# A selective-scan and spectral-filter kernel: z by halves in the turns' PSUM bank, conv ahead of it, later state copies, an own buffer for single h tiles, the image loaded first

## The chip, the core and the metric

The kernel runs on one core of one Trainium2 chip. The metric is the device time of one execution in microseconds (us); smaller is better. Three executions of the kernel before took 7441.77, 7444.82 and 7446.32 us, so its median is 7444.82 us. One more execution was profiled.

## The reference, cut to what matters

Two layers follow each other on x of shape 4 x 128 x 128 x 128 (batch, channel, height, width), all in float32. The first layer is a selective scan over the 16,384 pixels of each image:

```python
h1 = relu(xf @ mlp_w1.T + mlp_b1);  xm = h1 @ mlp_w2.T + mlp_b2
x_in, z = split(xm @ in_proj_w.T)                 # 256 channels each
u = silu(causal_conv(x_in, conv_w) + conv_b)      # 4 taps, depthwise
dt, B, C = split(u @ x_proj_w.T)                  # 8, 16, 16
delta = softplus(dt @ dt_proj_w.T + dt_proj_b)
h = h * exp(delta * A) + delta * B * u            # 16 states for each channel, step by step
y = (sum over states of h * C) + u * D
out = (y * silu(z)) @ out_proj_w.T
x1 = silu(group_norm(out)) + x
```

The second layer computes four softmax weights for each image from a normalised 1x1 convolution of x1, and filters x1 with a weighted sum of four spectral filters in the Fourier domain. It is matrix products with DFT matrices here, and the change doesn't touch its loop.

## The kernel before, in words

**Stages.** `block0` does the first layer and, for images 0 to 2, the softmax weights; `block1` does the rest. By the trace the scans of `block0` run from 61.0 to 6614.4 us, so what follows is `block1` and takes some 830 us.

**Chunks, units, slots.** `block0` cuts the four images into 128 chunks of 512 pixels. The 256 channels x 16 states of a chunk are 32 scans of 128 rows x 512: 8 units (`u`, numbered 0 to 7 in a chunk; two halves j of the channels, four rotations r) of four scans p = 0 to 3. Two scans are a pair and take one slot; a chunk is 16 slots. A unit's even slot scans p = 0 and 1 and its odd slot p = 2 and 3.

**One unit.** GpSimd makes `hb` = delta u B for p = 1 to 3 (`dbu`, L358); TensorE turns p = 0 into PSUM bank `b0` (L378); ScalarE makes the decay tiles `da0` to `da3` by Exp (`exps`, L391; `da1` to `da3` have one PSUM bank each, `da0` two SBUF buffers); VectorE runs the four scans (L409). For p = 2 and 3 VectorE scans in place in `da` and multiplies by C itself (L411). For p = 0 and 1 it scans into an SBUF tile `h` of two rows, of which there are two buffers, and GpSimd multiplies by C (L416). In a few units the share differs by `by_vector`: in the chunks in which the last image is normalised (48 of 128, "norming" chunks), GpSimd also takes p = 2 of unit 6, which needs an `h` tile in which one row is used; in every other of the remaining chunks VectorE takes p = 1 of unit 6. ScalarE copies the last state of each scan for the next chunk (L412 out of `da`, L417 out of `h`). TensorE sums `hb` over the states into `y` (L430).

**The order.** Nothing is scheduled automatically: `todo[slot, phase]` lists functions, and the program is written slot by slot, phase by phase, so each engine's queue is that order. `pre(k)` gives the slots of the steps that prepare chunk k, relative to the start of the chunk before it. Those that matter here, with their slots in a chunk:

- 9: `h1_mm`, 10: `h1_act`, 11: `xm_mm`, 12: `xm_act` (of the chunk after the next)
- 13 (written -3): `z_mm`, two products (L220) into two banks of the PSUM pool `psp`, which has two banks; 15 (-1): `z_act`, two copies (L225)
- 0 and 1: `cv_mm(0)`, `cv_mm(1)`, the convolution as 4 products each (L231; 8 in the profile, since a float32 product shows as two), in `psp`
- 2: `silu_act`: Silu of the convolution to `u` (L236, two instructions) and of z (L237, one)
- 3: `xd_mm` (L242) into the bank `pt`; 4: `xd_act`; 5: `dt_mm`; 6: `dt_act`, Softplus (L270); 5 to 14: turns of `du` in `pt` and `bt_act` (L299)

`pt` is the "turns' bank", a pool of one bank, `turn_bank`. Exp, Silu and Softplus need different tables, so ScalarE loads a table ahead of `silu_act`, ahead of `dt_act`, and ahead of the exps after each. `exps(n)` stands in slot n - 1. `dt_act` and `silu_act` stand between the exps of one unit's p = 2, 3 and the exps of the next unit's p = 0, 1.

**Start.** Twenty-five constants are loaded by L75 alternately on SyncE's and ScalarE's queues, and the taps (L124), before anything else; the first image tile (L191) follows on SyncE's queue, in memory that the taps had held.

**Images done.** `finish` normalises image b and computes its weights while image b + 1 is scanned; the last agg tiles (i from 28 on) use the turns' bank in slot 15 (`agg_mm`, L597, and `agg_act`, L601).

Of the kernel before, what the change touches and what calls it, by code (L numbers as in the profile page):

```python
# [33 lines left out]
P = 128  # L34
# [10 lines left out]
@with_exitstack  # L45
def kernel(ctx: ExitStack, tc: tile.TileContext, a: dict, out: bass.AP):
    nc = tc.nc
    x = a["x"]
    B, C, H, W = x.shape
    L = H * W  # L50
    NCH = L // T
    DI = a["mlp_w1T"].shape[1]
    NH = DI // P
    NS = (a["x_wT"].shape[1] - a["dt_wT"].shape[0]) // 2
    NG = NS // SQ
    ND = P // DG
    R = a["dt_wT"].shape[0]
    NX = R + 2 * NS
    KC = a["conv_wT"].shape[0]
    HALO = KC - 1  # L60
    WF = W // 2 + 1
    NF = a["wg_wT"].shape[1]

    cpool = ctx.enter_context(tc.tile_pool(name="const", bufs=1))
    dpool = ctx.enter_context(tc.tile_pool(name="dram", bufs=1, space=DRAM))
    spool = ctx.enter_context(tc.tile_pool(name="stats", bufs=2))
    opool = ctx.enter_context(tc.tile_pool(name="outs", bufs=2, space=DRAM))

    loads = [0]

    def const(name, shape, src):
        t = cpool.tile(shape, F32, tag=name, name=name)
        eng = (nc.sync, nc.scalar)[loads[0] % 2]
        loads[0] += 1
        eng.dma_start(out=t, in_=src)  # L75
        return t

    def col(name):

        n = a[name].shape[0] // P  # L80
        return const(name, [P, n], a[name].rearrange("(j p) -> p j", p=P))

    w1 = const("w1", [P, DI], a["mlp_w1T"])
    b1 = col("mlp_b1")
    w2 = const("w2", [P, NH, C], a["mlp_w2T"].rearrange("(j p) c -> p j c", p=P))
    b2 = col("mlp_b2")
    win = const("win", [P, 2 * DI], a["in_wT"])
    cb = col("conv_b")
    wx = const("wx", [P, NH, NX], a["x_wT"].rearrange("(j p) r -> p j r", p=P))
    wdt = const("wdt", [R, DI], a["dt_wT"])  # L90
    bdt = col("dt_b")
    alog = const("alog", [P, NH * NG * ND], a["alog_q"])
    sel = const("sel", [P, DG], a["c_sel"])
    dvec = col("D")
    wo = const("wo", [P, NH, C], a["out_wT"].rearrange("(j p) c -> p j c", p=P))
    gnw = col("gn_w")
    gnb = col("gn_b")
    ident = const("ident", [P, P], a["c_ident"])
    g0 = const("g0", [P, P], a["c_g0"])
    g1 = const("g1", [P, P], a["c_g1"])  # L100
    gam = col("gn_gamma")
    bet = col("gn_beta")
    wagg = const("wagg", [P, 2, C], a["agg_wT"].rearrange("(j p) o -> p j o", p=P))
    bagg = col("agg_b")
    wwg = const("wwg", [P, NF], a["wg_wT"])
    bwg = const("bwg", [P, NF], a["wg_b"].partition_broadcast(P))
    resw = const("resw", [P, 1], a["residual_weight"].partition_broadcast(P))

    eps = cpool.tile([P, 1], F32, tag="eps", name="eps")
    nc.vector.memset(eps, EPS)  # L110
    ones = cpool.tile([P, P], F32, tag="ones", name="ones")
    nc.vector.memset(ones, 1.0)

    amat = cpool.tile([P, NH * NG * ND], F32, tag="amat", name="amat")
    nc.scalar.activation(amat, alog, AF.Exp)
    nc.vector.tensor_scalar_mul(amat, amat, -1.0)
    diag = cpool.tile([P, NH, P], F32, tag="diag", name="diag")
    for j in range(NH):
        nc.vector.tensor_scalar_mul(diag[:, j, :], ident, dvec[:, j : j + 1])

    wck = cpool.tile([P, KC, DI], F32, tag="wck", name="wck")
    with tc.tile_pool(name="taps", bufs=1) as taps:
        cwb = taps.tile([P, KC, DI], F32, tag="cwb", name="cwb")
        nc.sync.dma_start(out=cwb, in_=a["conv_wT"].partition_broadcast(P))  # L124
        for t in range(KC):
            nc.vector.tensor_mul(wck[:, t, :], win[:, 0:DI], cwb[:, t, :])

    weff0 = cpool.tile([P, C], F32, tag="weff0", name="weff0")
    nc.vector.tensor_scalar_mul(weff0, wagg[:, 0, :], gam[:, 0:1])
    nc.vector.scalar_tensor_tensor(weff0, wagg[:, 1, :], gam[:, 1:2], weff0, ALU.mult, ALU.add)  # L130
    bias0 = cpool.tile([P, 1], F32, tag="bias0", name="bias0")
    wts = [cpool.tile([P, NF], F32, tag=f"wts{b}", name=f"wts{b}") for b in range(B)]

    x1 = [dpool.tile([C, H, W], F32, tag=f"x1_{b}", name=f"x1_{b}") for b in range(B)]
    x1flat = [t.rearrange("c h w -> c (h w)") for t in x1]
    xflat = x.rearrange("b c h w -> b c (h w)")

    stats, outs = {}, {}
    shared = SimpleNamespace(**{k: v for k, v in locals().items() if k not in ("ctx", "tc")})
    block0(tc, shared)  # L140
    block1(tc, shared)


def block0(tc, s):
# [4 lines left out]
    with ExitStack() as ctx:  # L149
# [18 lines left out]

        pb0 = psum("bias0")
        for j in range(2):  # L170
            nc.tensor.matmul(pb0[:, 0:1], s.wagg[:, j, :], s.bet[:, j : j + 1], start=j == 0, stop=j == 1)
        nc.vector.tensor_add(s.bias0, pb0[:, 0:1], s.bagg)

        st = {}
# [6 lines left out]
        def pre(k):  # L181
# [7 lines left out]
            def load():  # L189
                xt = d["xt"] = p1.tile([P, T], F32, tag="xt", name=f"xt_{k}")  # L190
                nc.sync.dma_start(out=xt, in_=s.xflat[b, :, i * T : (i + 1) * T])  # L191

# [22 lines left out]

            def z_mm():
                for j in range(NH):
                    ps["z", j] = psum(f"z_{k}_{j}")
                    w = s.win[:, DI + j * P : DI + (j + 1) * P]
                    nc.tensor.matmul(ps["z", j], w, d["xm"][:, HALO:], start=True, stop=True)  # L220

            def z_act():
                d["zs"] = p2.tile([P, NH, T], F32, tag="zs", name=f"zs_{k}", bufs=3)
                for j in range(NH):
                    nc.scalar.copy(d["zs"][:, j, :], ps["z", j])  # L225

# [83 lines left out]
            def rep_load(j):  # L310
# [7 lines left out]
                (-9, "pe", load), (-7, "pe", h1_mm), (-6, "act", h1_act), (-5, "pe", xm_mm), (-4, "act", xm_act),  # L318
                (-3, "pe", z_mm), (-1, "act", z_act), (0, "pe", partial(cv_mm, 0)), (1, "pe", partial(cv_mm, 1)),
                (2, "act", silu_act), (3, "pe", xd_mm), (4, "act", xd_act), (5, "pe", dt_mm), (5, "pe", xd_turn),  # L320
# [72 lines left out]
        def scans(n):  # L393
# [8 lines left out]
            last = d["last", j, r, p] = tiny.tile([P, 2], F32, tag=f"st{j}_{r}_{p}", name=f"st_{k}_{j}_{r}_{p}")  # L402
            if pool:
                h = p2.tile([P, 2, T], F32, tag="h", name=f"h_{k}_{j}_{r}_{p}")
            for q in range(2):
                b = hb[:, p + q, :] if p + q else d.pop("b0")
                init = 0.0 if k % NCH == 0 else st[k - 1]["last", j, r, p][:, q : q + 1]
                o = das[q] if q in dve else h[:, q, :]
                nc.vector.tensor_tensor_scan(o, das[q], b, init, ALU.mult, ALU.add)  # L409
# [3 lines left out]
            if pool:  # L413
                q = slice(pool[0], pool[-1] + 1)
                ps = slice(p + pool[0], p + pool[-1] + 1)
                nc.gpsimd.tensor_tensor(hb[:, ps, :], h[:, q, :], d["C"][:, ps, :], ALU.mult)  # L416
                nc.scalar.copy(last[:, q], h[:, q, T - 1])  # L417

# [47 lines left out]
        for k in range(n_chunks):  # L466
            for at, phase, f in pre(k) + post(k):
                todo[at + (k - 1) * NP, phase].append(f)
        io = SimpleNamespace(big=p2, bufs=3, small=tiny, psum=psum)

# [4 lines left out]
        def agg(i):  # L475
# [3 lines left out]
            c = i * NP  # L479
            return c + 9, c + 15, c + 15, turn_bank  # L480

# [12 lines left out]
        with tc.manual_schedule():  # L494
            for n in range(min(slots), max(slots) + 1):
                for phase in ("turn", "sums", "pe", "exps", "act", "pool", "dbu", "gate", "scans", "dve", "end"):
                    for f in todo[n, phase]:
# [3 lines left out]
def group_norm(s, io, b, mat, which, stat, at, then):  # L501
# [12 lines left out]
    def mean_mm():  # L514
        ps = g["ps"] = io.psum(f"gm_{which}_{b}")
        nc.tensor.matmul(ps[:, 0:1], mat, g["mv"][:, 0:1], start=True, stop=True)

# [7 lines left out]
    def var_mm():  # L525
        ps = g["ps"] = io.psum(f"gv_{which}_{b}")
        nc.tensor.matmul(ps[:, 0:1], mat, g["q"], start=True, stop=True)

# [13 lines left out]
def finish(s, io, b, first, norm, agg):  # L542
# [89 lines left out]

    todo = group_norm(s, io, b, s.g0, 0, lambda: stats[b], first, start)
    for i in range(NCH):
# [5 lines left out]
    c = at[2] + 5  # L640
    todo += group_norm(s, io, b, s.g1, 1, lambda: g["stat"], c, middle)
    todo += [(c + 4, "pe", bias_mm), (c + 4, "act", bias_act)]
    for i in range(NCH):
        at = agg(i)
        todo += [
            (at[0], "dve", partial(agg_load, i)), (at[1], "pe", partial(agg_mm, i, at[3])),
            (at[2], "act", partial(agg_act, i)),
        ]
# [321 lines left out]
```

## Time and profile before

| what | value |
|---|---|
| median of 3 executions | 7444.82 us (7441.77 to 7446.32) |
| profiled execution, its own time | 7446.74 us |
| its span, first to last instruction | 7445.0 us |
| mean granted TensorE clock | 0.875 |
| first scan starts, last scan ends | 60.97, 6614.41 us |
| first h1 product starts (L196) | 17.08 us |
| chunks 12 to 15, first scan to first scan | 49.62, 51.15, 50.42, 50.20 us |
| a norming chunk (34 to 48), first scan to first scan | 52.0 us |

The profile's engines are PE (TensorE matmul), PEld (its weight loads), DVE (VectorE), ACT (ScalarE), POOL (GpSimd) and SP (SyncE). In a timeline row stand the start, the time it took, engine, line, operation, output <- inputs, shapes and count, and in brackets the idle time of the engine before it with the instruction that is taken to have released it. Where an instruction waits for several semaphores, the profile names the one that came last by its records, which may be another's. Vector instructions overlap a little: a scan is 1.26 us long, but the next starts 1.18 us after it; a product is 0.67 us long and the next starts 0.59 us after it.

### The profile page before, as it was taken

The numbers are of one execution on the slowest core, as the hardware profiler recorded it, in microseconds if no ns is written. First come the engines' busy times: TensorE is split into PE (matmuls) and PEld (weight loads), VectorE is DVE, ScalarE is ACT, GpSimd is POOL, SyncE is SP. The second block draws the span as 40 slices with busy tenths as digits, with TensorE's granted clock in tenths as the row PEclk, the third lists the DMA queues.
The fourth block names the chain that finished last, engine by engine and source line by source line (L and its number), as shares of the span: only waits on it lengthen the run. The fifth ranks groups of instructions, "written<-read, shape, count | busy, mean of one in ns | idle before, by whom it ended". The sixth has DMA issues, their size and how long they took to land.

```text
span 7445.0 us, 90541 instructions
## 1 busy us (share of the span) xinstructions
PE 6005.7 (81%) x25908; PEld 2664.1 (36%) x25908; DVE 7031.4 (94%) x8168; ACT 6328.6 (85%) x13181; POOL 6900.6 (93%) x3188
## 2 busy tenths in 40 slices
PE   7787878877778788887777788877777788867999
PEld 2223223322222233332222223232222233237999
DVE  6999999999999999999999999999999999977787
ACT  6888888888888888888888888888888888866887
POOL 6999999999999999999999999999999999976788
PEclk8888888888888888888888889988888889889999
DMA  4444444444554544544545454445554554547665
GB/s 138 159 154 150 151 156 156 143 161 168 174 188 164 179 165 156 169 166 169 184 168 185 161 171 166 159 165 175 171 188 166 173 169 151 173 149 216 177 185 155
DMA packets 853767, 1242.06 MB, mean 167 GB/s; under 512 B 76680, under 2 KB 308240, under 8 KB 853264
## 3 DMA queue, kind: packets, MB, share of 16 engines
q1 hardware_dynamic: 851152, 1236.11, 50.3%
q8 instruction: 204, 3.34, 0.2%
q14 instruction: 299, 2.45, 0.1%
q10 hardware_dynamic: 2112, 0.16, 0.0%
HBM read 992.71 MB, written 243.27 MB: 166 GB/s over the span
## 4 chain that ended last, share of the span: by engine, by line
ACT 20%; DVE 19%; PE 17%; POOL 9%; issue 8%; DMA 5%; SPq 1%; DVEq 0%; ACTq 0%; POOLq 0%
DVE da L409 8%; ACT da L391 8%; DVE h L409 6%; PE pp_cv L231 5%; ACT bt L299 4%; POOL hb L358 4%; POOL hb L416 4%; DVE hb L411 3%; DMA dd<-delta 2%; PE y L430 2%; PE pa L776 1%; ACT L391 1%; PE px L790 1%; PE px L791 1%; POOL du L307 1%
## 5 line engine op out<-in xcount | busy, mean ns | idle before, releaser
L358 POOL TENSOR_TENSOR hb<-rdu,rB 128x1536 f32<-128x1536 f32 (+2 forms) x1536 | 3607.6, 2365 | 16.2 <-DMA rdu<-dd 16.2
L416 POOL TENSOR_TENSOR hb<-h,rC 128x1024 f32<-128x1024 f32 (+1 forms) x1072 | 2438.7, 2277 | 279.8 <-DVE h L409 263.0
L391 ACT ACTIVATE da<-rdelta,amat 128x512 f32<-128x512 f32 x4096 | 2674.6, 696 | 9.2 <-ACT st L412 0.2
L409 DVE TENSOR_TENSOR_SCAN da<-da,st,hb 128x512 f32<-128x512 f32 x1976 | 2420.3, 1268 | 7.1 <-ACT da L391 7.0
L378 PE MATMUL b<-ident,bt 128*128 128x128 f32 x4096 | 768.9, 311 | 767.9 <-DVE h L409 633.0
L430 PE MATMUL y<-hb,sel 128*32 128x512 f32 x8192 | 1364.0, 743 | 4.8 <-POOL hb L416 2.9
L409 DVE TENSOR_TENSOR_SCAN h<-da,st,b 128x512 f32<-128x512 f32 x992 | 1261.3, 1271 | 111.4 <-POOL hb L358 37.5
L411 DVE TENSOR_TENSOR hb<-da,rC 128x512 f32<-128x512 f32 x2040 | 1296.7, 674 | 3.0
L409 DVE TENSOR_TENSOR_SCAN h<-da,st,hb 128x512 f32<-128x512 f32 x1000 | 1252.7, 1256 | 1.3 <-ACT da L391 1.3
L299 ACT ACTIVATE bt<-pt_dut,xdt 128x256 f32<-128x256 f32 x2048 | 1194.6, 708 | 46.8 <-PE pt_dut L288 46.5
L231 PE MATMUL pp_cv<-xm,wck 128*128 128x512 f32 x2048 | 1111.7, 692 | 9.8 <-ACT zs L225 9.7
L378 PEld LDWEIGHTS b<-ident,bt 128*128 128x128 f32 x4096 | 532.0, 156 | 1341.4 <-DVE h L409 997.1
L412 ACT COPY st<-da 128x1 f32<-128x1 f32 x2040 | 295.8, 173 | 567.9 <-DVE hb L411 562.6
L231 PEld LDWEIGHTS pp_cv<-xm,wck 128*128 128x128 f32 x2048 | 438.4, 226 | 771.1 <-issue 502.8
L755 POOL TENSOR_TENSOR wb<-wb,term 128x1040 f32<-128x1040 f32 x192 | 460.9, 2401 | 157.2 <-ACT term L749 147.2
L288 PE MATMUL pt_dut<-ident,du 128*128 128x128 f32 x1024 | 214.1, 337 | 280.5 <-ACT st L412 271.4
L426 PE MATMUL y<-u,diag 128*128 128x512 f32 x512 | 291.0, 651 | 156.8 <-DVE zs L440 155.6
L307 POOL TENSOR_TENSOR du<-delta,u 128x512 f32<-128x512 f32 x256 | 319.0, 1267 | 37.5 <-ACT delta L270 37.5
L417 ACT COPY st<-h 128x2 f32<-128x2 f32 (+1 forms) x1072 | 214.7, 200 | 162.8 <-DVE h L409 154.6
L288 PEld LDWEIGHTS pt_dut<-ident,du 128*128 128x128 f32 x1024 | 134.1, 164 | 578.6 <-POOL du L307 419.2
L196 PE MATMUL pp_h<-xt,w 128*128 128x512 f32 x512 | 296.6, 707 | 51.7 <-DMA xt<-in_x 46.6
L391 ACT ACT_TABLE_LOAD x261 | 334.9, 1283 | 2.9
(137 smaller groups left out, 8019.0 us busy)
## 6 DMA issues: line engine op xcount, KB each, us to landing
rdelta<-dd SPq DMA_DIRECT2D x1024, 256.0 KB, 3.6
rdu<-dd SPq DMA_DIRECT2D x1024, 256.0 KB, 4.6
rC<-bc SPq DMA_DIRECT2D x512, 256.0 KB, 5.1
rB<-bc SPq DMA_DIRECT2D x384, 256.0 KB, 3.5
dd<-delta SPq DMA_DIRECT2D x256, 256.0 KB, 5.3
dd<-du SPq DMA_DIRECT2D x256, 256.0 KB, 4.5
ft<-in_filt_w SPq DMA_DIRECT2D x96, 520.0 KB, 7.1
xt<-in_x SPq DMA_DIRECT2D x128, 256.0 KB, 5.5
```

The costliest lines, as they stand in the source:

```text
L231: nc.tensor.matmul(ps["cv", j], w, d["xm"][:, t : t + T], start=t == 0, stop=t == KC - 1)
L288: nc.tensor.transpose(ps["dut"][:, 2 * t + j, :], d["du"][:, j, at : at + P], s.ident)
L299: nc.scalar.activation(d["bt"][:, 2 * h + t, :, :, q], src, AF.Copy, scale=d["xdt"][:, 2 * h + t, R + q : R + q + 1])
L307: nc.gpsimd.tensor_tensor(du, d["delta"][:, j, :], d["u"][:, j, :], ALU.mult)
L358: nc.gpsimd.tensor_tensor(hb[:, p : p + n, :], d["du", j][:, m : m + n, :], d["B"][:, p - 1 : p - 1 + n, :], ALU.mult)
L378: nc.tensor.transpose(b[:, t * P : (t + 1) * P], src, s.ident)
L391: nc.scalar.activation(d["da", p][q], d["delta", j][:, m, :], AF.Exp, scale=s.amat[:, c : c + 1])
L409: nc.vector.tensor_tensor_scan(o, das[q], b, init, ALU.mult, ALU.add)
L411: nc.vector.tensor_tensor(hb[:, p + q, :], das[q], d["C"][:, p + q, :], ALU.mult)
L416: nc.gpsimd.tensor_tensor(hb[:, ps, :], h[:, q, :], d["C"][:, ps, :], ALU.mult)
L430: nc.tensor.matmul(y[m * DG : (m + 1) * DG, :], s.sel, d["hb", j, r][:, p, :], start=False, stop=r == NG - 1)
L755: nc.gpsimd.tensor_tensor(wb, wb, u[n].terms[f], ALU.add)
```

## The change

- `z_mm` and `z_act` are split into halves j. Both halves use the turns' bank, one after the other: `z_mm(0)` in slot 15, `z_act(0)` in slot 0, `z_mm(1)` in slot 1, `z_act(1)` in slot 2 ahead of `silu_act`. `cv_mm(0)` moves from slot 0 to 13, `cv_mm(1)` from 1 to 15, ahead of `z_mm(0)`.
- The copies of last states out of `h` (L417) go to a phase "late" of the next slot, behind that slot's exps. Those out of `da` (L412) stay.
- An `h` tile of one row gets a buffer `h1` of its own, and the ring of two keeps the tiles of two rows.
- All constants are loaded on SyncE's queue. The first image tile is loaded on ScalarE's, behind `w1` in the program; then come the constants and products that the scan needs (the first slot's end), in slot 4 those of the normalisation, in slot 8 the products made of these. The taps are loaded into `wck` and multiplied in place.
- The agg steps in the turns' bank move from slot 15 to the end of slot 0 of the next chunk.
- The small tiles of `finish` come in `block0` from a pool with one buffer.

```diff
             def load():
                 xt = d["xt"] = p1.tile([P, T], F32, tag="xt", name=f"xt_{k}")
-                nc.sync.dma_start(out=xt, in_=s.xflat[b, :, i * T : (i + 1) * T])
+                (nc.sync if k else nc.scalar).dma_start(out=xt, in_=s.xflat[b, :, i * T : (i + 1) * T])
...
+            def z_mm(j):
+                ps["z", j] = turn_bank(f"z_{k}_{j}")
+                w = s.win[:, DI + j * P : DI + (j + 1) * P]
+                nc.tensor.matmul(ps["z", j], w, d["xm"][:, HALO:], start=True, stop=True)
+
+            def z_act(j):
+                if j == 0:
+                    d["zs"] = p2.tile([P, NH, T], F32, tag="zs", name=f"zs_{k}", bufs=3)
+                nc.scalar.copy(d["zs"][:, j, :], ps["z", j])
...
-                (-3, "pe", z_mm), (-1, "act", z_act), (0, "pe", partial(cv_mm, 0)), (1, "pe", partial(cv_mm, 1)),
+                (-3, "pe", partial(cv_mm, 0)), (-1, "pe", partial(cv_mm, 1)), (-1, "pe", partial(z_mm, 0)),
+                (0, "act", partial(z_act, 0)), (1, "pe", partial(z_mm, 1)), (2, "act", partial(z_act, 1)),
...
-            if pool:
+            if len(pool) == 2:
                 h = p2.tile([P, 2, T], F32, tag="h", name=f"h_{k}_{j}_{r}_{p}")
+            elif pool:
+                h = p1.tile([P, 1, T], F32, tag="h1", name=f"h1_{k}_{j}_{r}_{p}")
...
-                nc.scalar.copy(last[:, q], h[:, q, T - 1])
+                todo[n + 1, "late"].append(partial(nc.scalar.copy, last[:, pool[0] : pool[-1] + 1], h[:, :, T - 1]))
...
-        io = SimpleNamespace(big=p2, bufs=3, small=tiny, psum=psum)
+        todo[min(n for n, _ in todo), "end"].append(partial(s.first_constants, s))
+        todo[4, "end"].append(partial(s.later_constants, s))
+        todo[8, "end"].append(partial(s.later_products, s, psum))
+        io = SimpleNamespace(big=p2, bufs=3, small=p1, psum=psum)
...
-            return c + 9, c + 15, c + 15, turn_bank
+            return c + 9, c + 16, c + 16, turn_bank
...
-                for phase in ("turn", "sums", "pe", "exps", "act", "pool", "dbu", "gate", "scans", "dve", "end"):
+                for phase in ("turn", "sums", "pe", "exps", "late", "act", "pool", "dbu", "gate", "scans", "dve", "end"):
...
-            (at[0], "dve", partial(agg_load, i)), (at[1], "pe", partial(agg_mm, i, at[3])),
-            (at[2], "act", partial(agg_act, i)),
+            (at[0], "dve", partial(agg_load, i)), (at[1], "end" if at[3] else "pe", partial(agg_mm, i, at[3])),
+            (at[2], "end" if at[3] else "act", partial(agg_act, i)),
```

`first_constants` loads, all on SyncE's queue and in this order: b1, w2, b2, win, the taps, cb, wx, wdt, bdt, ident, alog, D, sel; then VectorE multiplies the taps, ScalarE makes exp of alog (`amat`), and VectorE negates it and makes `diag`. `later_constants` loads the other twelve; `later_products` holds the two instructions of `weff0`, the two small products of `bias0` and its sum.

## The prediction, made blind

> **What bounds the kernel now.** First the page's busy line:
>
> ```profile
> PE 6005.7 (81%) x25908; PEld 2664.1 (36%) x25908; DVE 7031.4 (94%) x8168; ACT 6328.6 (85%) x13181; POOL 6900.6 (93%) x3188
> ```
>
> VectorE and GpSimd are both nearly full, ScalarE isn't. By the busy time in stretches VectorE works 1552.7 of the 1587 us from 1813 to 3400: in the scans VectorE sets the pace. So I read what VectorE waits for between 130 and 6500 us:
>
> ```profile
> DVE h L409 <- POOL hb L358: 39.2, 47, 1.3
> DVE h L409 <- POOL du L307: 35.2, 122, 0.6
> DVE h L409 <- POOL hb L416: 30.3, 45, 0.7
> ```
>
> Three groups, each at one place of the chunk. The releaser named is in doubt for the first two, so I took ScalarE's timeline of chunk 14, then VectorE's:
>
> ```profile
> 773.07 0.16 ACT L412 COPY st<-da 128x1 f32<-128x1 f32 x1 [0.44 <-DVE hb L411]
> 773.13 1.31 ACT L391 ACTIVATE da<-rdelta,amat 128x512 f32<-128x512 f32 x2
> 774.46 1.28 ACT L236 ACT_TABLE_LOAD   x1
> 775.75 0.69 ACT L236 ACTIVATE u<-pp_cv,conv_b 128x512 f32<-128x512 f32 x1
> 777.30 0.69 ACT L236 ACTIVATE u<-pp_cv,conv_b 128x512 f32<-128x512 f32 x1 [0.87 <-PE pp_cv L231]
> 777.89 1.05 ACT L237 ACTIVATE zs<-zs 128x1024 f32<-128x1024 f32 x1
> 778.84 0.18 ACT L417 COPY st<-h 128x2 f32<-128x2 f32 x1
> 779.02 1.28 ACT L391 ACT_TABLE_LOAD   x1
> 780.32 1.30 ACT L391 ACTIVATE da<-rdelta,amat 128x512 f32<-128x512 f32 x2
> ```
> ```profile
> 778.86 1.27 DVE L411 TENSOR_TENSOR hb<-da,rC 128x512 f32<-128x512 f32 x2
> 781.13 1.28 DVE L409 TENSOR_TENSOR_SCAN h<-da,st,b 128x512 f32<-128x512 f32 x1 [1.00 <-POOL hb L358]
> ```
>
> The scan opens unit 2. It starts 0.09 us after the first of the two exps of 780.32 ends (780.32 + 0.72): its releaser is ScalarE. That queue starts when VectorE frees `da2` and `da3` (773.07) and goes without a pause through two exps, Silu's table, `silu_act`, a state copy, Exp's table and the exp, but for 0.87 us in which it waits for the second convolution. The second product of 778.86 starts at 779.45, so the scan was due 0.59 later, at 780.04: it is 1.09 us late.
>
> The second group is the same in slot 6 to 8 round Softplus, in every chunk (0.28 us idle, with the lost overlap 0.37 late):
>
> ```profile
> 2528.35 1.26 ACT L270 ACTIVATE delta<-pp_dt,dt_b 128x512 f32<-128x512 f32 x2
> 2529.51 0.19 ACT L417 COPY st<-h 128x2 f32<-128x2 f32 x1
> 2529.72 1.28 ACT L391 ACT_TABLE_LOAD   x1
> 2531.01 1.30 ACT L391 ACTIVATE da<-rdelta,amat 128x512 f32<-128x512 f32 x2
> ```
>
> The third is GpSimd's indeed, in norming chunks, at the opening of unit 7:
>
> ```profile
> 2549.06 0.69 DVE L411 TENSOR_TENSOR hb<-da,rC 128x512 f32<-128x512 f32 x1
> 2550.41 1.28 DVE L409 TENSOR_TENSOR_SCAN h<-da,st,b 128x512 f32<-128x512 f32 x1 [0.66 <-POOL hb L416]
> ```
> ```profile
> 2548.03 3.58 POOL L416 TENSOR_TENSOR hb<-h,rC 128x1024 f32<-128x1024 f32 x2
> ```
>
> The single `h` of unit 6 took the ring's second buffer, so unit 7 needs the one that the first of these two products reads until 2550.38.
>
> **Own buffer for single tiles.** Unit 7 then gets the buffer of unit 5, read long before. The scan could start at 2549.06 + 0.59 = 2549.65, 0.76 us earlier, in 45 chunks (34 to 48 of each of three images): 34 us. What is late next would be GpSimd. It waits 1.9 us for `h` in such a chunk (1.74 and 0.16, in the timeline after 2520), so its work is 50.1 of 52.0 us; VectorE would need 51.2. Its `hb` of the next chunk's unit 0 is made at 2503.0 for a scan at 2505.5, that of unit 1 at 2508.7 for one at 2511.4: 2.5 us in hand, of which 0.76 goes. In even unnormed chunks the single tile isn't there, in odd ones nothing waits for it. I take 34; the bounds are 0, if GpSimd's lag returns it, and 34.
>
> **Copies behind the exps.** In slots 0, 4, 6 and so on a copy moved changes only ScalarE's own idle time, since the exps behind it wait for VectorE anyway. On the path are the copies of slots 2 and 6. At 778.84 zs ends at 778.94 and the table load starts at 779.02: 0.08 us. At 2529.51 delta ends at 2529.62, the load starts at 2529.72: again 0.08, after a normal start. The copy comes later, behind exps, and nothing is near that needs it (the next chunk does). Slot 6: 0.08 x 128 = 10 us. Slot 2 is in the next sum. Bounds: 0 and 0.2 (its whole length) in each.
>
> **Convolution ahead, z in halves.** The gain is the wait for the second convolution: the second u starts 777.30 - 775.75 = 1.55 us after the first where 0.59 is usual (chunk 15): 0.97 us. The price is `z_act(1)`: two z copies used to stand in slot 15, where nothing was late; one now stands in slot 2 between exps and Silu's table, on the path. L225's median is 599 ns, two start 0.48 apart; between an exp and a table load it adds some 0.52. `z_act(0)` in slot 0 is hidden: ScalarE idled 0.99 us there ahead of the state copy. So in chunk 14: from 773.13 to 781.13 are 8.00 us; - 0.97 - 0.08 + 0.52 = 7.47; the scan would start at 780.60, 0.56 late instead of 1.09. But the wait for the convolution isn't in every chunk. Counted chunk by chunk, of four unnormed ones in a row it is 0.85, 0.87, 0 and 0.06 us, and the scan is 1.08, 1.09, 0.11 and 0.28 late (periods 51.15, 50.42, 50.20, 49.62). Every one becomes 0.56: mean 0.64 before, 0.56 after, 0.08 x 80 unnormed chunks = 6 us. In norming chunks ScalarE has 1.5 us more to do there (two norm Silus) and VectorE 2.4 (four operations of 0.6), so the chain has 0.8 in hand; it needs 0.44 of it: 0.
>
> [...] The row has the 1283 and the next ACTIVATE 0.01 us behind it (774.46, 1.28, 775.75). [...] PE busy 4.05 of 7.50 us from 705.5 to 713, then a granted clock of 0.50 until 719.3; L231 takes 592 ns at the median and up to 1223. This speaks for and against. `cv_mm(0)` in slot 13 keeps PE busy 1.4 us longer ahead of the slow stretch, but slots 2 and 3 lose their convolution and become idle. At the full clock (L231's products follow each other by 0.43) `cv_mm(1)` starts 1.5 us before a chunk's first scan and ends 1.9 after it, z(0) 2.8, b0 of unit 1 3.3, the sums 4.1, z(1) 5.2; `z_act(1)` wants it at 7.3, the scan wants b0 at 5.9. One slow window adds 1.7 us, which fits; two, as chunk 14 and its like have now, don't, and cost some 0.7. I put two at one chunk in ten: 80 x 0.1 x 0.7 = 6 us lost. In slots 3 to 5 a slow window delays b0 of unit 3, turned four us ahead, by 1.7: hidden. Sum of this part 6 - 6 = 0, between -39 (z(1) hidden after all: 0.56 x 70) and +30.
>
> **The agg steps.** Eleven times ScalarE waits 23.4 us in all for the product in slot 15, and VectorE is late by 0.2 to 1.3 in slot 1. Behind exps(1) the same wait stands before exps(2), with z(0) and `cv_mm(1)` ahead on PE: a lateness of 0 to 1.5 us at unit 1. I take 4 us gained of 8; the least is -5.
>
> **Start.** The first h1 product starts at 17.08, because SyncE waits for the taps' memory (L191 issues at 14.31). The image would be issued at 0.8, and after the 2.7 us of before land at 3.5. Then ScalarE waits: amat's exp stands in its queue ahead of `h1_act` and needs alog, the twelfth load of SyncE's queue. The twelfth went out at 7.84 us there before, and ident took 2.6 to land: exp at 10.4, `h1_act` 10.7 against 19.17. Behind the convolution z(0), z(1) and Silu's table no longer hide: some 3.5 back. So 5, bounds 2 and 12; and chunk 0's own waits (2.2 and 1.4 us idle) give perhaps 2. Twelve loads in slot 4 hold SyncE's queue some 6 us; queued behind are rB, rC, the delta and du stores, whose replicas are wanted over 10 us later. `later_products` and memsets cost VectorE 1 us: -1.
>
> **Sum.** 34 + 10 + 0 + 4 + 7 - 1 = 54 us off the profiled execution's 7446.74, which is 1.9 over the median: 7393, or **7391** for the median. `block1` stays.
>
> **Rivals.** *z's second copy is hidden*, or the chain starts earlier than I think, and unit 2 is never late: 39 us more, 7352. For it: ScalarE idles 1.98 us in slot 1. Against: it idles for VectorE's `da`, ahead of exps(3). Chance 0.19. *GpSimd takes the place of the `h` wait*: 93% busy against VectorE's 94. Then 34 come back: 7425. Against: the 1.9 us it waits. Chance 0.14, half of it with start and copies failing too, within 0.2%. *Slower*: with one bank, z(1) waits for z(0)'s copy and PE's slow clock, and `z_act(1)` makes Exp wait in slot 2. If z(1) ends x us after the 7.3, it costs 80x + 48(x - 0.36), and the rest gives 54: it decides from x = 0.6 on, z(1) at 7.9 in every chunk, where I have 5.2 to 6.9. At x = 1.2 it is 136 - 54 = 82 more: 7527. Chance 0.05. The forecast itself has 0.62, between 7365 and 7412.
>
> The range 7340 to 7425 leaves out the slower case, half of GpSimd's and the far end of the first. About 0.2%, 15 us, can be told from no change: faster 0.89, within 0.06, slower 0.05.
>
> **What would show it.** Right: no idle time named L416 before VectorE's scans; norming chunks at 51.2 us; no wait of u (L236) for L231; a copy of zs between exps and Silu's table, and unit 2's scan late by some 0.5 in every unnormed chunk, whose mean stays near 50.2; Softplus's place at 0.20 idle; the first scan at 56. Wrong: u's table load waiting for a z product, idle time at unit 1, VectorE waiting for `hb` in slots 0 to 4.

## The result and the profile after

The kernel after takes 7432.29 us (median of 22 runs, 7419.65 to 7443.19) against 7440.71 us (22 runs on the same chip) of the kernel before: ratio 0.9988, 95% interval 0.9982 to 0.9993. That is 8 us gained; the forecast was 54 (7391), and its range ended at 7425, 7 us short. The profiled execution took 7436.28 us, span 7434.2 us, mean granted clock 0.894.

What VectorE waits for between 130 and 6500 us, kernel after:

```profile
DVE h L409 <- POOL hb L356: 45.2, 54, 1.5
DVE h L409 <- POOL du L304: 24.3, 120, 0.4
...
DVE h L409 <- PE y L429: 9.4, 9, 2.9
DVE lg L620 <- PE pp_lg L615: 8.1, 2, 4.1
DVE h L409 <- POOL hb L415: 0.9, 2, 0.5
```

L356, L304 and L415 were L358, L307 and L416. The third group of before is gone (30.3 to 0.9), the second has shrunk (35.2 to 24.3). The first, unit 2's scan, has grown from 39.2 to 45.2, and two groups are new. Two of those left out here grew as well: waits put down to exps (1.3 to 10.3, 13 of 16 at unit 1) and to "issue" (5.5 to 10.3, at unit 2). What is new on ScalarE stands in its waits for the same stretch:

```profile
ACT zs L222 <- PE pt_z L217: 277.4, 124, 4.2
```

ScalarE waits for a z product in nearly every chunk, 2.2 us in the mean. By stages of the two profiled executions (first scan to first scan, as in the table of before):

| stage | before, us | after, us | gain | forecast |
|---|---|---|---|---|
| first scan starts | 60.97 | 55.77 | 5.2 | 5 |
| chunks 0 to 2 | 152.3 | 156.8 | -4.5 | 2 - 1 |
| 45 norming chunks (34 to 48, and the same 15 of the next two images) | 2341.9 | 2303.7 | 38.2 | 34 + 4 |
| 63 unnormed chunks | 3174.7 | 3187.6 | -12.9 | 0 + 5 |
| 11 chunks with an aggregation step in slot 0 (61 to 64, 93 to 96, 125 to 127) | 558.4 | 573.2 | -14.8 | 4 + 1 |
| six chunks in which a normalisation begins or ends (33, 49 and so on), and what follows the last scan | 1156.8 | 1157.1 | -0.3 | 0 |

(The second numbers in the last column are the copies' 10 us, by chunk; the gains add up to 10.9 us, the spans differ by 10.7.) The gains came. The part thought to be worth nothing, z by halves, lost in two rows.

**Own buffer.** In chunk 48 GpSimd's product of unit 6's single `h` still runs while VectorE opens unit 7; the scan no longer waits for it. VectorE, then GpSimd:

```profile
2541.18 0.69 DVE L411 TENSOR_TENSOR hb<-da,rC 128x512 f32<-128x512 f32 x1
2541.79 1.27 DVE L409 TENSOR_TENSOR_SCAN h<-da,st,b 128x512 f32<-128x512 f32 x1
```
```profile
2540.26 3.58 POOL L415 TENSOR_TENSOR hb<-h,rC 128x1024 f32<-128x1024 f32 x2
```

The scan starts 0.61 us after the product ahead of it started, 1.35 before.

**Copies.** Softplus of the same chunk: the second delta ends at 2521.81 and the load starts at 2521.84. The copy that used to stand between them is gone, and the scan of that place idles 0.20 instead of 0.28 us:

```profile
2520.55 1.26 ACT L267 ACTIVATE delta<-pp_dt,dt_b 128x512 f32<-128x512 f32 x2
2521.84 1.28 ACT L389 ACT_TABLE_LOAD   x1
```

**z by halves.** ScalarE in chunk 13, whose first scan starts at 718.08:

```profile
718.27 1.30 ACT L389 ACTIVATE da<-rdelta,amat 128x512 f32<-128x512 f32 x2
722.82 0.58 ACT L222 COPY zs<-pt_z 128x512 f32<-128x512 f32 x1 [3.24 <-PE pt_z L217]
723.30 1.31 ACT L389 ACTIVATE da<-rdelta,amat 128x512 f32<-128x512 f32 x2
724.53 0.18 ACT L500 COPY st<-h 128x2 f32<-128x2 f32 x1
724.62 0.22 ACT L412 COPY st<-da 128x1 f32<-128x1 f32 x2
724.81 1.30 ACT L389 ACTIVATE da<-rdelta,amat 128x512 f32<-128x512 f32 x2
726.05 0.58 ACT L222 COPY zs<-pt_z 128x512 f32<-128x512 f32 x1
726.64 1.28 ACT L233 ACT_TABLE_LOAD   x1
```

The wait isn't where the forecast looked. The second copy (726.05) finds z(1) ready and puts 0.53 us between the end of exps(3) (726.11) and Silu's table load, as forecast (0.52). The first copy stands idle for 3.24 us, and behind it queue exps(2), the state copies, exps(3) and Silu's table. exps(3) start 6.73 us after the chunk's first scan. Here exps(n) are those of slot n, so exps(2) are unit 1's first and exps(3) its last. Chunk 15, whose first scan starts at 819.74:

```profile
822.82 0.59 ACT L222 COPY zs<-pt_z 128x512 f32<-128x512 f32 x1 [1.59 <-PE pt_z L217]
...
825.75 0.16 ACT L412 COPY st<-da 128x1 f32<-128x1 f32 x1 [0.43 <-DVE hb L411]
825.80 1.31 ACT L389 ACTIVATE da<-rdelta,amat 128x512 f32<-128x512 f32 x2
```

Here the same wait is 1.59 us and costs nothing: exps(3) start at 6.06, set by VectorE (the copy ahead of them waited for it). VectorE idles 0.97 us ahead of unit 2's scan in chunk 13 and 0.46 in chunk 15:

```profile
732.26 1.28 DVE L409 TENSOR_TENSOR_SCAN h<-da,st,b 128x512 f32<-128x512 f32 x1 [0.97 <-POOL hb L356]
```
```profile
833.26 1.28 DVE L409 TENSOR_TENSOR_SCAN h<-da,st,b 128x512 f32<-128x512 f32 x1 [0.46 <-issue]
```

PE's timeline tells the two apart, first chunk 13, then 15:

```profile
716.71 5.21 PE L228 MATMUL pp_cv<-xm,wck 128*128 128x512 f32 x8
721.76 1.02 PE L217 MATMUL pt_z<-xm,win 128*128 128x512 f32 x2
```
```profile
818.22 3.70 PE L228 MATMUL pp_cv<-xm,wck 128*128 128x512 f32 x8
821.76 1.02 PE L217 MATMUL pt_z<-xm,win 128*128 128x512 f32 x2
```

The convolution ahead of z(0) takes 5.21 us in one and 3.70 in the other. In windows of 3.41 us (columns: us, PE busy and instructions, granted clock, DMA share, GB/s) the clock of chunk 13 is halved in the one that covers its first scan:

```profile
712.96:716.37 3.41, 1.60 (x12) 1.00 0.37 128
716.37:719.78 3.41, 3.41 (x8) 0.50 0.93 305
```

Counted over the 63 unnormed chunks, 28 have a half-clock window near the first scan (from 3.2 us before it to 1.5 after). All 28 are late by 0.90 us or more at unit 2, and 12 of them also at unit 1, by 0.34 or more. Of the 35 others 32 are late by 0.46 and three by 0.70 to 0.80. (From here on "late" is the idle time ahead of the scan; the prediction adds the lost overlap, 0.09 us more.)

**Aggregation.** The agg product wants the same bank as z(0), so on PE it waits for z(0)'s copy, ahead of `b0` of unit 1; ScalarE then waits for it in turn. PE in chunk 61 (first scan 3158.17), then ScalarE, then VectorE:

```profile
3164.45 1.13 PE L599 MATMUL pt_agg<-x,weff 128*128 128x512 f32 x2 [0.68 <-ACT zs L222]
```
```profile
3163.81 0.58 ACT L222 COPY zs<-pt_z 128x512 f32<-128x512 f32 x1 [4.15 <-PE pt_z L217]
3165.61 0.66 ACT L603 ACTIVATE pt_agg<-pt_agg,bv 128x512 f32<-128x512 f32 x1 [1.22 <-PE pt_agg L599]
...
3166.29 1.29 ACT L389 ACTIVATE da<-rdelta,amat 128x512 f32<-128x512 f32 x2
```
```profile
3167.09 1.28 DVE L409 TENSOR_TENSOR_SCAN h<-da,st,b 128x512 f32<-128x512 f32 x1 [2.94 <-PE y L429]
```

Two waits in a row, 5.37 us, and unit 1's scan is 2.94 us late. It starts just after the first exp of 3166.29 (which ends at 3167.01), so ScalarE releases it, not the y products that the profile names.

These waits are not most of what the eleven chunks lost. VectorE's idle time at unit 1 is 9.8 us in all of them, but 8.2 in slot 1 went with the old place of the step. At unit 2 it rose from 3.8 to 10.7 us, as in the unnormed chunks. And 8.1 are new, in chunks 64 and 96: the logits (L615, L620) of the image just finished. Their slot is counted from the last aggregation step, so they moved with it, from slot 4 to 5, where `dt_mm` stands ahead of them and fills both banks of `psp` until Softplus reads them. VectorE, then PE, in chunk 64:

```profile
3339.38 0.16 DVE L620 SCALAR_TENSOR_TENSOR lg<-pp_lg,bwg 128x4 f32<-128x4 f32 x1 [4.08 <-PE pp_lg L615]
```
```profile
3338.75 0.59 PE L615 MATMUL pp_lg<-wwg,pbc 128*128 128x4 f32 x2 [3.35 <-ACT delta L267]
```

### The profile page after: what moved, and what is told of

It reads as the page before. It is cut to its first block, busy times and chain, and to the rows that moved or that the text cites. A ratio compares the mean times of both kernels' runs of the same rounds, so it can differ in the third digit from the quotient of the medians.

```text
span 7434.2 us, 90798 instructions
## 1 busy us (share of the span) xinstructions
PE 5942.1 (80%) x25908; PEld 2603.6 (35%) x25908; DVE 7034.7 (95%) x8168; ACT 6298.4 (85%) x13181; POOL 6901.4 (93%) x3188
## 4 chain that ended last, share of the span: by engine, by line
ACT 34%; DVE 23%; PE 23%; issue 9%; POOL 6%; DMA 4%; SPq 1%; DVEq 0%; ACTq 0%; POOLq 0%
ACT da L389 14%; DVE da L409 11%; DVE h L409 7%; PE pp_cv L228 6%; ACT bt L296 6%; DVE hb L411 4%; PE y L429 3%; POOL du L304 3%; ACT L389 2%; POOL hb L415 2%; ACT zs L222 2%; DMA dd<-delta 2%; ACT u L233 2%; ACT zs L234 1%; PE pa L778 1%
## 5 line engine op out<-in xcount | busy, mean ns | idle before, releaser
L356 POOL TENSOR_TENSOR hb<-rdu,rB 128x1536 f32<-128x1536 f32 (+2 forms) x1536 | 3607.9, 2365 | 16.9 <-DMA rdu<-dd 16.9
L415 POOL TENSOR_TENSOR hb<-h,rC 128x1024 f32<-128x1024 f32 (+1 forms) x1072 | 2436.4, 2275 | 271.8 <-DVE h L409 256.7
L429 PE MATMUL y<-hb,sel 128*32 128x512 f32 x8192 | 1345.7, 734 | 2.9 <-POOL hb L415 2.7
L228 PE MATMUL pp_cv<-xm,wck 128*128 128x512 f32 x2048 | 986.1, 625 | 21.3 <-ACT xm L212 12.1
L412 ACT COPY st<-da 128x1 f32<-128x1 f32 x2040 | 288.3, 174 | 509.6 <-DVE hb L411 504.4
L425 PE MATMUL y<-u,diag 128*128 128x512 f32 x512 | 348.9, 769 | 334.7 <-DVE zs L439 334.7
L228 PEld LDWEIGHTS pp_cv<-xm,wck 128*128 128x128 f32 x2048 | 383.5, 198 | 648.5 <-issue 515.3
L222 ACT COPY zs<-pt_z 128x512 f32<-128x512 f32 x256 | 149.3, 583 | 294.5 <-PE pt_z L217 294.5
L304 POOL TENSOR_TENSOR du<-delta,u 128x512 f32<-128x512 f32 x256 | 319.2, 1268 | 32.5 <-ACT delta L267 32.5
```

Source lines behind the costliest of these rows:

```text
L228: nc.tensor.matmul(ps["cv", j], w, d["xm"][:, t : t + T], start=t == 0, stop=t == KC - 1)
L304: nc.gpsimd.tensor_tensor(du, d["delta"][:, j, :], d["u"][:, j, :], ALU.mult)
L356: nc.gpsimd.tensor_tensor(hb[:, p : p + n, :], d["du", j][:, m : m + n, :], d["B"][:, p - 1 : p - 1 + n, :], ALU.mult)
L415: nc.gpsimd.tensor_tensor(hb[:, ps, :], h, d["C"][:, ps, :], ALU.mult)
L429: nc.tensor.matmul(y[m * DG : (m + 1) * DG, :], s.sel, d["hb", j, r][:, p, :], start=False, stop=r == NG - 1)
```

## The experiments

Theory: z(0) reaches ScalarE late, because it is queued on PE behind the second convolution and PE's clock is halved there, to 0.50, in 28 of the 63 unnormed chunks; ScalarE's queue then holds back exps(2) and exps(3). Rival: the second z copy between the exps and Silu's table is the whole price. Each kernel stood beside the kernel before on the same chip; us gained or lost are the ratio's distance from 1 times the time before, and times by stage are those of the profiled executions.

**1. Everything but z** (the kernel after with z, convolution and aggregation where they were).

```diff
-(-3, "pe", partial(cv_mm, 0)), (-1, "pe", partial(cv_mm, 1)), (-1, "pe", partial(z_mm, 0)),
-(0, "act", partial(z_act, 0)), (1, "pe", partial(z_mm, 1)), (2, "act", partial(z_act, 1)),
+(-3, "pe", z_mm), (-1, "act", z_act), (0, "pe", partial(cv_mm, 0)), (1, "pe", partial(cv_mm, 1)),
...
```

> Everything of the change except z and the convolution, which stay as before (and the agg steps with them). Theory: the buffer, the later copies and the start gain as forecast (38 us in norming chunks, 0.16 in each of 63 unnormed ones, 5 at the start), and z with the convolution gives them back; so 7440 - 53 = about 7387. Rival, GpSimd or another wait returns the gain of the other parts: it stays near the change's 7432.

7398.43 us, ratio 0.9942 (0.993 to 0.9954): 43 us gained. Against the kernel after, whose ratio is 0.9988, z costs 34 us. By stages of the profiled executions its price is 4.8 us of the start (first scan 50.98), 17.4 in the unnormed chunks and 12.4 in the aggregation's; the other stages together give back 3.6.

**2. z alone** (the kernel before with z, the convolution and the aggregation's move only).

> Only z by halves in the turns' bank, the convolution ahead, and the agg steps' move, on the kernel before. Theory: ScalarE waits in slot 0 for z(0), which PE has queued behind the second convolution, and that makes unit 1 or unit 2 late: 63 unnormed chunks x 0.35 + 15 in the agg chunks + 5 in the first ones = 42 slower, about 7483; norming chunks keep 52.0. Rival (this part is neutral, as forecast): 7441.

7493.36 us, ratio 1.0068 (1.0055 to 1.0082): 51 us lost. Alone it is dearer than inside the change: 37 of 63 unnormed chunks have the half clock near their first scan, and in 12 of them unit 1's scan is late by 1.04 us or more (in the kernel after 7 of 28 are, by 0.95 to 1.00).

**3. Own buffer alone.**

```diff
-if pool:
+if len(pool) == 2:
     h = p2.tile([P, 2, T], F32, tag="h", ...
+elif pool:
+    h = p1.tile([P, 1, T], F32, tag="h1", ...
...
```

> Only the own buffer for single h tiles (and the small tiles of the normalisation in a pool with one buffer, without which it doesn't fit), on the kernel before. Both the forecast and the theory: 45 chunks x 0.76 = 34 us, 7407, norming chunks at 51.3. Rival (GpSimd's lag returns it): 7441.

7412.29 us, ratio 0.9959 (0.9947 to 0.9971): 31 us, where 34 were forecast. Norming chunks take 51.27 us.

**4. The copies alone.**

> The kernel before with one part of the change alone: the copies of the last states of GpSimd's h stand behind the next pair's exps. The forecast's term: 0.08 us in each of 128 Softplus slots and 0.08 at unit 2 where it is late: 10 to 15 us, 7431. If the copy is hidden behind the table load or comes back as a later wait, 7445.

7435.41 us, ratio 0.9988 (0.9982 to 0.9995): 9 us, where 10 were forecast. But not where forecast: the 45 norming chunks take 2341.9 us, as before. Softplus's place gains its 0.08 us there, and unit 7's wait for GpSimd grows by as much (30.2 us in 40 waits for 30.3 in 45). With the own buffer that wait is gone and the gain stays: 51.27 us in experiment 3, 51.19 in the kernel after.

**5. The start alone.**

> The kernel before with the start of the change alone: image loaded first, taps multiplied in place, later constants in slots 4 and 8. First scan at about 51 instead of 61 us: 7435. If the later loads delay the replicas of the first chunks, or the first chunks give the gain back: 7445.

7437.58 us, ratio 0.9992 (0.9984 to 1.0): 6 us, with an interval that reaches no change. The first scan starts at 49.22 us, 11.75 earlier. Chunk 0 takes 55.79 us instead of 50.30; most of the difference is `later_products`, 4.6 us of VectorE's time in it: see the last section.

The three parts, 31 + 9 + 6, make 46 us; together (experiment 1) they make 43. They add up, and what is missing is z.

**6. More work for PE** (the kernel after; two products of the first convolution are computed twice in slot 13, the first time to be overwritten).

```diff
 ps["cv", j] = psum(f"cv_{k}_{j}")
+for t in range(2 if j == 0 else 0):
+    w = s.wck[:, t, j * P : (j + 1) * P]
+    nc.tensor.matmul(ps["cv", j], w, d["xm"][:, t : t + T], start=True, stop=True)
```

> The kernel after, but the first two of the four products of the first convolution are computed twice in slot 13 (the first copy is overwritten at once), 1.7 us more PE work at full clock, so that PE is not idle ahead of slot 15. If z(0) is late because PE's clock is granted at half around the chunk's first scan in about half of the chunks, those chunks become like the others: about 63 unnormed chunks gain 0.4 us (26 us) and the eleven aggregation steps 6 us: about 7400, and no unnormed chunk opens with a clock of 0.5. If the clock isn't the cause, the products only add work: 7432 or more.

7407.74 us, ratio 0.9948 (0.9935 to 0.996): 30 us faster than the kernel after, with 1.7 us more work in each chunk. None of the 63 chunks has the half clock near its first scan, and 59 are late by 0.46 us at unit 2 (the other four by 0.70 to 0.96). The window ahead of chunk 13's first scan (715.17) is busy for 3.03 us, and the next one keeps the clock:

```profile
710.05:713.46 3.41, 3.03 (x16) 1.00 0.39 112
...
713.46:716.87 3.41, 3.41 (x12) 1.00 0.92 306
```

The unnormed chunks take 25.5 us less, as the theory said (26). So in the 28 chunks it is the half clock that makes z(0) too late: with more work for PE, but at the full clock, the loss is gone.

**7. z(0) one place earlier on PE.**

```diff
-... (-1, "pe", partial(cv_mm, 1)), (-1, "pe", partial(z_mm, 0)),
+... (-1, "pe", partial(z_mm, 0)), (-1, "pe", partial(cv_mm, 1)),
```

> The kernel after, but z(0) is issued ahead of the second convolution in slot 15, one place of PE's queue earlier; z(1) and both copies stay where they are. If ScalarE's wait for z(0) in slot 0 is the cause, the wait goes, every unnormed chunk has unit 2's scan some 0.5 us late and none 1.0, and unit 1's scan is in time: 16 us in the unnormed chunks and some 8 in the aggregation steps: about 7408. If the second copy is the cause, nothing changes: 7432.

7411.68 us, ratio 0.9952 (0.9939 to 0.9964). The total is near the expectation, for other reasons than those given. ScalarE's wait for z falls from 277.4 to 23.7 us, and the aggregation's chunks gain 11 and the start 5. The unnormed chunks gain 10 instead of 16: 31 have the half clock, and 20 of these are still late by 0.69 us or more, now because the convolution, which takes 4.27 us in chunk 51, stands ahead of `b0` of unit 1 and of z(1):

```profile
2640.47 2.08 PE L217 MATMUL pt_z<-xm,win 128*128 128x512 f32 x2
2642.34 4.27 PE L228 MATMUL pp_cv<-xm,wck 128*128 128x512 f32 x8
2646.45 0.60 PE L376 MATMUL b<-ident,bt 128*128 128x128 f32 x4
```

**8. The second copy one slot earlier** (slot 1, ahead of exps(3)).

```diff
-... (2, "act", partial(z_act, 1)),
+... (1, "act", partial(z_act, 1)),
```

> The kernel after, but the copy of z(1) stands in slot 1, ahead of exps(3), instead of slot 2. If the late z(0) is the main cause, chunks at full clock gain 0.46 us (z(1) is there in time) and those with a half clock lose about as much, since z(1) then ends later than exps(3) could start: 7432, 10 either way. If the second copy between the exps and Silu's table is the whole cause, every unnormed chunk gains 0.5: about 7400.

7478.49 us, ratio 1.0044 (1.003 to 1.0057): 42 us slower than the kernel after, outside the expectation. The sign in the half-clock chunks was right and their loss too small: the copy waits again for z(1), now ahead of exps(3). In chunk 19 (first scan 1032.41):

```profile
1037.14 0.59 ACT L222 COPY zs<-pt_z 128x512 f32<-128x512 f32 x1 [3.25 <-PE pt_z L217]
...
1039.63 0.59 ACT L222 COPY zs<-pt_z 128x512 f32<-128x512 f32 x1 [0.59 <-PE pt_z L217]
...
1040.31 1.30 ACT L389 ACTIVATE da<-rdelta,amat 128x512 f32<-128x512 f32 x2
```

exps(3) start 7.90 us after the first scan, 1.17 later than in the kernel after, and 36 chunks instead of 28 have the half clock. Of the 27 chunks at full clock ten gain most of what was expected (0.11 to 0.13 late at unit 2), but eleven others are late by 1.00 to 1.08: there the second convolution starts only 0.6 us ahead of the first scan on PE, not 1.5, and z(0) and z(1) come 0.9 later without any half clock. The rival, by which every chunk should have gained, falls.

**9. Both orders repaired** (z(0) ahead of the second convolution, z(1) in slot 0 right behind it, its copy in slot 1; the aggregation at the end of slot 1).

```diff
-(0, "act", partial(z_act, 0)), (1, "pe", partial(z_mm, 1)), (2, "act", partial(z_act, 1)),
+(0, "act", partial(z_act, 0)), (0, "pe", partial(z_mm, 1)), (1, "act", partial(z_act, 1)),
...
```

> The changed kernel with z(0) ahead of the second convolution on PE in slot 15, z(1) behind it in slot 0, z's second copy in slot 1 in place of 2, and the agg steps at the end of slot 1. Theory: z(0) is ready when ScalarE comes to copy it, the second copy lies in the time in which ScalarE waits for VectorE, so unit 2 is late by 0.1 to 0.3 in place of 0.56 to 1.07: 63 x 0.75 = 47, and some 12 in the agg chunks, from 7432 to about 7373. Rival (the loss is the convolution's two banks held from slot 13 to 2, or PE's slow clock as such): the same as the changed kernel, 7432.

7381.05 us, ratio 0.9915 (0.9902 to 0.9929). Unit 2's scan is late in one unnormed chunk of 63. Unit 1's is late by 0.07 us or more in 26 of the 29 chunks with the half clock, by up to 1.7:

```profile
DVE h L409 <- PE b L376: 17.1, 15, 1.7
```

**10. The same with more work for PE**, and the aggregation moved to slot 4.

> The fourth kernel (z(0) ahead of the second convolution, z(1) and its copy a slot earlier) with the two repeated products of the fifth in slot 13, and the aggregation's last step moved from slot 1 to slot 4. What the fourth kernel still loses is b0 of unit 1 in chunks with two half-clock windows (up to 1.7 us in about one chunk in eight) and 1.3 us in each of eleven aggregation steps: 18 and 10 us, so about 7353 if the half clock is what delays b0; 7381, as without the products, if it isn't, less up to 10 for the aggregation step.

7373.06 us, ratio 0.9904 (0.989 to 0.9917), 20 us above the expectation. The unnormed chunks gain 19 us, as expected (18): 49.3 and 50.04 us by turns, with nothing late but the Softplus place in all but one. The aggregation loses 4.7 us instead of gaining 10. Its wait at unit 2 is gone (14.2 us to 0.4), but in slot 4 its product stands on PE behind those of xd and of the output: in chunk 93 ScalarE waits 1.60 us for xd and 2.19 for it, and unit 3's scan is 1.86 late. So 6.6 us come at unit 3 and 8.8 at Softplus's place, and the logits wait 8.3 us in place of 3.7. And the repeats in chunk 0 cost the start 3.7.

**11. The aggregation out of the turns' bank** (in slots 12 and 13, where the pool `psp` has a bank free; no repeats in chunk 0, and its z(1) in slot 1).

```diff
-return c + 9, c + 20, c + 20, turn_bank
+return c + 9, c + 12, c + 13, None
...
```

> The eighth kernel, with two repairs: the aggregation's late tiles are multiplied in slot 12 and rectified in slot 13, in one of the two rotating banks instead of the turns' bank (free there between the copy of xm and the second convolution), and chunk 0 neither repeats products nor has z(1) a slot early. If the turns' bank is what makes the aggregation late, its eleven chunks fall from 51.8 to about 50 (20 us), and the start gets back 3.7 us of repeats and 4.8 us: 7373 - 28 = 7345. If it is only the work of the aggregation step on ScalarE, the eleven stay near 51.5: 7363.

7342.11 us (7339.94 to 7342.94), ratio 0.9863 (0.9849 to 0.9876). The aggregation's chunks take 49.54 us, 24.7 less in all eleven. Of these 7.3 are the logits, which move with the step, to slot 2, and wait 1.0 us instead of 8.3; what the free bank gives by itself isn't shown, since slot, bank and logits moved together. This kernel is the fastest of all, 102 us below the kernel before. What VectorE still waits for between 130 and 6500 us:

```profile
DVE h L413 <- POOL du L307: 25.3, 123, 0.4
DVE rstd L539 <- ACT rstd L536: 13.1, 6, 2.8
DVE h L413 <- ACT da L393: 1.3, 3, 0.4
```

**12. The same without the repeats.**

> The ninth kernel without the repeated products: what is left is the order z(0), second convolution, z(1) with the aggregation repaired. If the half clock costs what the fourth kernel showed against the eighth (0.24 us in 29 and 0.35 us in 34 chunks, 19 us), 7345 + 19 = 7364; if moving the aggregation also moves the clock's slow stretches out of the way, 7345.

7361.6 us, ratio 0.989 (0.9876 to 0.9903). 27 chunks have the half clock again, and 26 of them open unit 1 late by 0.07 us or more. The repeats add 1.7 x 127 = 216 us of work to PE and take 20 us off the time.

## Why the prediction was wrong, step by step

- **Own buffer, 34.** Right: 38 in norming chunks with the copies' share of 4, and 31 when tried alone. GpSimd didn't take the wait's place; it had the slack that was read from its timeline.
- **Copies, 10.** Right: 0.28 to 0.20 us in every chunk. That they gave 9 alone is in part luck: in norming chunks, where 4 were counted, they gave nothing without the own buffer.
- **z by halves, "`z_act(0)` in slot 0 is hidden".** This is the step that failed. It was priced by ScalarE's idle time in the kernel before, 0.99 us, and not by when z(0) is there. The forecast had worked that out: z(0) ends 2.8 us after the first scan at full clock, one slow window adds 1.7 (an estimate: half of a window of 3.41 us; the convolution of chunk 13 took 5.21 - 3.70 = 1.51 us longer than chunk 15's). At 4.5 the copy, exps(2), the state copies and exps(3) no longer fit: in chunk 13 exps(3) start 1.99 us after the copy, and in chunk 15, where VectorE sets their start, they start at 6.06, so the copy may start at 4.07 at the latest. It starts at 4.74. Only `b0` and `z_act(1)` were tested against one slow window ("which fits"); the first copy in the queue wasn't.
- **"Two at one chunk in ten."** With it fell the count, the author's estimate. One slow window is enough, and it was there in 28 chunks of 63, not 6. What was forecast for a full-clock chunk, 0.56 late, came: 0.46 idle is 0.55 late as the forecast counts. But the mean of the 63 was 0.78 (before 0.68), 14 us more than at 0.56, and 7 us of idle time at unit 1 came on top. Idle time at unit 1 is the one of the forecast's signs of being wrong that appeared.
- **Aggregation, +4.** Wrong in sign: -14.8. Of 8 us of waits 4 were to stay, and 9.8 came: the forecast saw z(0) and the convolution ahead of it, but not that the product also waits for z(0)'s copy out of the same bank, so that one late z(0) makes two waits. Some 7 more came at unit 2, as in the unnormed chunks. And the logits, which moved along, had no term at all: 8.1. Its "least", -5, was too narrow.
- **Start, 5 + 2 - 1.** The first scan moved by 5.2, which is luck in part: the loads give 10.0 in experiment 1 and 11.75 in experiment 5 (why they differ is open) where 8.5 were worked out, and z takes 4.8 back, not 3.5. The term of 1 us for `later_products` was mis-sized: its two products took 4.6, and chunks 0 to 2 lost 4.5 us where 1 gained was forecast.
- **The slower rival** named the right kind of thing, z and PE's slow clock before a copy that Exp stands behind, but at the wrong copy: it asked for z(1) at 7.9 us, and z(1) was in time. "z's second copy is hidden" fell too (0.46 us in every full-clock chunk), and came true in experiments 9 to 12, where z(1) and its copy stand a slot earlier and z(0) comes ahead of the second convolution.
- **The sum.** The forecast's start term holds 3.5 us lost to z. Without z it has 34 + 10 + 10.5 - 1 = 53.5, and experiment 1 measured 43 (chunks 0 to 2 make some 5 of the difference); z with the aggregation it put at 4 - 3.5, and they cost 34. So 9 us are left of 54. The z part was bounded by 39 us gained and 30 lost in the unnormed chunks, where it cost 17; the aggregation, bounded apart at 5 lost, cost 12 against experiment 1, and the start 5.

The half clock itself is not new: by the same count the kernel before has it near the first scan in all 63 chunks and experiment 1 in 62, where z's products stand in slot 13 and its copies in slot 15. New is that ScalarE waits for a z product at that place.

What stays open: why z alone meets the half clock in 37 chunks and inside the change in 28. The chunks' lengths differ, so the windows may fall differently; no run shows it.

## What to carry to other kernels

A step moved onto an in-order queue costs what it waits for there (3.24 us in chunk 13), not its own length (0.58): for each moved instruction work out when its operand is ready, at the slowest clock seen (0.50 here), and what is queued behind it, before calling it hidden by idle time. A bank handed from user to user makes every later user wait for the reader of the one before (0.68 us on PE and then 1.22 on ScalarE in chunk 61). Steps whose place is counted from a moved step move with it: the logits, one slot later, cost 8.1 us. Where PE isn't the bound but its latency is, look at the granted clock of the very window in which the product is wanted (0.50 at chunk 13's first scan), not at its mean (0.894).

## What the runs showed of the hardware

**The granted clock changed on a grid of 3.413 us, in chunk 13 after a window that was half idle.** Every change of the granted clock in the kernel after lies on a grid of 3.413 us, within 4 ns over 7434 us, whatever the chunk does. Chunks 13 and 15 issue the same work; chunk 13's first scan lies 1.71 us after a grid point and chunk 15's 0.97, and so the window ahead holds 1.60 us of PE work in one and 2.17 in the other (window 815.36 to 818.78):

```profile
815.36:818.78 3.42, 2.17 (x14) 1.00 0.57 187
818.78:822.19 3.41, 3.41 (x10) 1.00 0.90 287
```

In these two chunks the window with 1.60 us of work was followed by a clock of 0.50, the one with 2.17 by 1.00. Over the whole trace 270 full-clock windows are followed by a half-clock one, with PE busy for 46% at the median; of those followed by another at full clock, 95% were busy for over 51%. Of the 269 half-clock windows after which the full clock came back, none was busy for under 82%. The busy share alone doesn't tell them apart: 46 of the 270 were over 90% busy, and what decides isn't shown. In the kernel before, the window ahead of chunk 13's half clock (709.06 to 712.47) held 0.55 us of PE work, and the two after it (to 719.30) ran at 0.50. The mean clock says little: in experiment 1 it is 0.857, and that kernel is 34 us faster than the kernel after with 0.894.

**The same VectorE instruction took 2.27 us instead of 0.29.** `later_products`' first product (128x128) took 0.29 us at the start of the kernel before, and in slot 8 of the kernel after 2.27, its second 2.36 instead of 0.34. VectorE, then GpSimd:

```profile
83.27 2.27 DVE L126 TENSOR_SCALAR weff<-wagg,gn_gamma 128x128 f32<-128x128 f32 x1
85.57 2.36 DVE L127 SCALAR_TENSOR_TENSOR weff<-wagg,gn_gamma,weff 128x128 f32<-128x128 f32 x1
```
```profile
82.01 3.44 POOL L356 TENSOR_TENSOR hb<-rdu,rB 128x1536 f32<-128x1536 f32 x1
85.42 2.36 POOL L415 TENSOR_TENSOR hb<-h,rC 128x1024 f32<-128x1024 f32 x1
```

Each ends 0.09 or 0.15 us after the GpSimd product that ran beside it (85.45 and 87.78). Why they took 2.27 and 2.36 us isn't shown; no run here tried it by itself.
